# Layer 0 of a four-layer convolutional block: the pixel transposes become products with a diagonal of scales, with a second product for the biases

## The chip, the core and the metric

The kernel runs on one core of a Trainium2 chip. The metric is the time of one execution on the device in microseconds, as the median of the runs shown. The core has five engines with a queue each: TensorE (PE in the profile; PEld are its weight loads), VectorE (DVE), ScalarE (ACT), GpSimd (POOL) and SyncE (SP, which here only issues DMAs).

## The reference, cut to what matters

The input x is one image of 1024 channels by 64 x 64 pixels in float32. Four layers each add their output to x, and each first normalizes its input over 32 groups of 32 channels (`_gn`). Layers 1 and 3 are products with a 1024 x 1024 matrix and a bias, layer 2 is three products around a scan over the pixels. Only layer 0 is touched in substance:

```
x_norm = _layernorm2d(_gn(x), ln_w, ln_b)      # per channel, over its 64 x 64 pixels
dt     = softplus(einsum('bsdc,c->bsd', x_norm, dt_w) + dt_b)
log_a  = dt * -exp(log_A)                      # per channel and image row
M      = exp(cums[t] - cums[j]) for j <= t     # cums: running sum over the channels
x      = x + einsum('btjr,bjrc->btrc', M, x_norm)
```

So layer 0 is, for every pixel, a linear recurrence over the 1024 channels, out[t] = a[t] out[t-1] + x_norm[t], in which a depends on the channel and on the image row. The two normalizations of a channel fold into one scale and one bias per channel; ln_w and ln_b are a scale and a bias per pixel.

## The kernel before

**Tiling of layer 0.** The image is taken in eight units u of two channel tiles (256 channels, one chunk c) by half the pixels (2048); u counts chunk 0 low half, chunk 0 high half, chunk 1 low half and so on. `low[c]` and `image` hold the halves in SBUF with channels on partitions. The recurrence runs along channels, so pixels must come to the partitions: a unit is cut into four pieces, and each piece i (32 in all) covers four tiles of 128 pixels by 256 channels.

**What happens to a piece.** `normalize(n)` on ScalarE writes the scaled and shifted channels of a quarter of a unit to a tile xn (L563; two calls for every two pieces). `turn_in(i)` transposes them with TensorE, eight 128 x 128 transposes with `ident` into two PSUM tiles (L578), and VectorE (L584) or ScalarE (L586) writes them to `XT[i]`, applying the pixel's ln_w and ln_b; the argument `share` says which of the four are VectorE's. `row_dt(i)` accumulates the products for dt of a unit in `PD[u]` (L594). `decay(u, step)` turns a finished PD into the factors `A[u]` (ScalarE L603 to L612, VectorE L609). `scan(i)` is four recurrences on VectorE (L620), `hand_on(i)` keeps the last column for the next chunk, `turn_back(i)` transposes back into PSUM (L634), and `add_up(i)` adds that to the image and keeps the sums (L644). `unit_stats` takes the statistics of a unit that is still to come (L542), `norm_chunk(c)` works out scale and bias of a chunk in steps with two small products (gn_pg L198, gn_pv L207), and `squares` takes sums of squares of the finished pixels on ScalarE (L659).

**The order.** It is written by hand: layer 0 runs under a manual schedule, so every engine executes its instructions in the order in which the Python text emits them. Before the loop, chunk 0 is normalized, seven pieces are turned in (LEAD = 7) and unit 0 gets its decay. Then piece i of the loop emits scan(i), add_up(i - 1), turn_in(i + 7), row_dt(i + 6), turn_back(i), with the statistics of later units in pieces 0 to 3 and 8 to 11 and the decay of the next unit in every fourth piece. The PSUM tiles of turn_in ("tp") and of turn_back ("pb") are double buffered; small products of the normalization use "tp" too. GpSimd meanwhile sums blocks of the weights of later layers (L445 to L448), with its own DMAs.

**Layers 1 and 2** use a Strassen-like scheme with seven products (L832) on sums of blocks: `b_sets` is a generator whose steps are spread between the products, plain blocks b21, b11, b22, then t1 = b12 - b11, t2 = b22 - t1, t3 = t2 - b11 and t4 = b21 - t2, each as four subtractions of 128 x 512 (L790), t2 on VectorE for the first pair and on GpSimd (or the engine given) for later ones. The products come in the order b21, b11, b22, t2, t3, t1, t4.

Of the kernel before, what the change touches and what calls it, by code (L numbers as in the profile page):

```python
# [9 lines left out]
F32 = mybir.dt.float32  # L10
# [8 lines left out]
P = 128  # L19
C = 1024  # L20
HW = 64
# [69 lines left out]
def tile_net(ctx: ExitStack, tc: tile.TileContext, x, par_d, cst_d, w_d, w2_d, dbcw_d, out):  # L91
# [5 lines left out]
    def ps_tp(name):  # L97
        return psum.tile([P, FB], F32, tag="tp", name=name)
# [57 lines left out]
    def finish_of(steps):  # L156

        while True:
            try:
                next(steps)  # L160
            except StopIteration as stop:
                return stop.value
# [336 lines left out]
    with tc.issue_after(exp_ln.ins), tc.tile_pool(name="l0x", bufs=2) as lx, \  # L499
# [7 lines left out]
        def half(u):  # L507

            c, h = divmod(u, 2)
            return image[:, c * CH : (c + 1) * CH, :] if h else low[c]  # L510
# [27 lines left out]
        def unit_stats(u, some):  # L538
            c, h = divmod(u, 2)
            for j in some:  # L540
                k, i = divmod(j, 4)
                nc.vector.bn_stats(stats[:, c * CH + k, 4 * h + i, :], half(u)[:, k, i * FB : (i + 1) * FB])  # L542
# [8 lines left out]
            nc.vector.tensor_scalar_mul(nmean0[:, at], mean, -1.0)  # L551
            norms[c] = yield from norm_steps(f"gn0_{c}", mean, var, CH, layernorm=True)

        xn, XT, PD, A, dt, PB = {}, {}, {}, {}, {}, {}

        def normalize(n):

            u, j = divmod(n, 4)
            q, k = divmod(j, CH)
            scale, bias = norms[u // 2]  # L560
            xn[n] = l0.tile([P, 2, TR, HW // 4], F32, tag=f"xn{k}", name=f"xn{n}")
            part = half(u)[:, k, :].rearrange("p (r a g w) -> p a g r w", r=TR, a=2, g=2)[:, q]
            nc.scalar.activation(xn[n], part, AF.Identity, bias=bias[:, k : k + 1], scale=scale[:, k : k + 1])  # L563

        def tile_in(u, t, k):
            v = xn[4 * u + CH * (t // 8) + k].rearrange("p g r w -> p (g r w)")
            return v.rearrange("p (g b j) -> p g j b", g=2, j=4)[:, t // 4 % 2, t % 4]

        def turn_in(i, share, tag="tp"):

            u, g = divmod(i, NPIECE)
            XT[i] = l0.tile([P, 4, CH * P], F32, tag="xt", name=f"xt{i}", bufs=10)
            for b in range(2):
                pt = (psum if tag == "tp" else ps0).tile([P, FB], F32, tag=tag, name=f"xpt{i}_{b}")
                for j in range(2):
                    t = 4 * g + 2 * b + j
                    for k in range(CH):
                        nc.tensor.transpose(pt[:, (CH * j + k) * P : (CH * j + k + 1) * P],  # L578
                                            tile_in(u, t, k), ident)
                for j in range(2):  # L580
                    at = (u % 2) * T0 + 4 * g + 2 * b + j
                    to, ps = XT[i][:, 2 * b + j, :], pt[:, j * CH * P : (j + 1) * CH * P]
                    if 2 * b + j in share:
                        nc.vector.tensor_scalar(to, ps, pcol("lnw", at), pcol("lnb", at), ALU.mult, ALU.add)  # L584
                    else:
                        nc.scalar.activation(to, ps, AF.Identity, bias=pcol("lnb", at), scale=pcol("lnw", at))  # L586

        def row_dt(i):
            u, g = divmod(i, NPIECE)
            if g == 0:  # L590
                PD[u] = ps0.tile([P, FB], F32, tag="pd", name=f"pd{u}")
            for j in range(4):
                t = 4 * g + j
                nc.tensor.matmul(PD[u][:, : CH * P], dtm[:, t, :], XT[i][:, j, :], start=(t == 0), stop=(t == T0 - 1))  # L594
# [42 lines left out]
        def add_up(i):  # L637
            u, g = divmod(i, NPIECE)
            c, h = divmod(u, 2)
            for k in range(CH):  # L640
                part = half(u)[:, k, :].rearrange("p (r g q j) -> p g r q j", r=TR, g=4, q=4)[:, g]
                at = h * NPIECE + g
                ps = PB[i][k].rearrange("p (j r q) -> p r q j", j=4, r=TR)
                nc.vector.scalar_tensor_tensor(part, ps, 1.0, part, ALU.mult, ALU.add,  # L644
                                               accum_out=sum0[:, c * CH + k, at : at + 1])

        def squares(u, j, g=None):

            c, h = divmod(u, 2)
            k, q = divmod(j, 2)  # L650
            ct = c * CH + k
            junk = l0.tile([P, HN // 2], BF16, tag="junk", name=f"junk{u}_{j}_{g}", bufs=1)
            if g is None:
                part, at = half(u)[:, k, q * HN // 2 : (q + 1) * HN // 2], h * NPIECE + q
            else:
                part = half(u)[:, k, :].rearrange("p (r w) -> p r w", r=TR)[:, :, 16 * g : 16 * g + 16]
                at = h * NPIECE + g
                junk = junk[:, :FB].rearrange("p (r w) -> p r w", r=TR)
            nc.scalar.activation(junk, part, AF.Square, bias=nmean0[:, ct : ct + 1], accum_out=sq0[:, ct, at : at + 1])  # L659

        sums = (None for m in (W1, WX) for _ in sum_weights(m, wsum0, nc.gpsimd, lag=(1, 0)))
# [11 lines left out]
            next(chain)  # L673
            score(4)
        finish_of(chain)
        for n in range(4):
            normalize(n)
        unit_stats(2, range(4))
        turn_in(0, range(4))
        turn_in(1, range(4), "pb")  # L680
        for _ in scores:
            pass
        row_dt(0)
        turn_in(2, (1, 3))
        row_dt(1)
        turn_in(3, (1, 3), "pb")
        row_dt(2)
        unit_stats(2, range(4, 8))
        unit_stats(3, range(4))
        row_dt(3)  # L690
        decay(0, 0)
        normalize(4)
        unit_stats(3, range(4, 8))
        chain = norm_chunk(1)
        decay(0, 1)
        decay(0, 2)
        next(chain)
        normalize(5)
        turn_in(4, ())
        next(chain)  # L700
        row_dt(4)
        next(chain)
        normalize(6)
        normalize(7)
        turn_in(5, ())
        row_dt(5)
        turn_in(6, ())
# [1 line left out]
                8: [(7, range(4))], 9: [(7, range(4, 8))], 10: [(6, range(4))], 11: [(6, range(4, 8))]}  # L709
        for i in range(NI):  # L710
            u, g = divmod(i, NPIECE)
            if i > 0 and i + LEAD + 2 < 4 * NU:
                normalize(i + LEAD + 2)
            scan(i)
            hand_on(i)
            if i == 0:
                finish_of(chain)
                chain = iter(())
            if g == 3 and u + 1 < NU:
                decay(u + 1, 1)  # L720
                decay(u + 1, 2)
            if i > 0:
                add_up(i - 1)
            if i + LEAD < NI:
                turn_in(i + LEAD, ())
            if i + LEAD - 1 < NI:
                row_dt(i + LEAD - 1)
            turn_back(i)
            if i == 0:
                normalize(LEAD + 1)  # L730
                normalize(LEAD + 2)
            if u + 1 < NU and g == 2:
                decay(u + 1, 0)
            for v, some in todo.get(i, ()):
                unit_stats(v, some)
            if i in (3, 11):
                chain = norm_chunk(2 if i == 3 else 3)
            next(chain, None)
            if i >= NPIECE:
                squares(u - 1, g)  # L740
            if u == NU - 1 and 0 < g:
                for k in range(CH):
                    squares(u, 2 * k, g - 1)
            if g == 0 and u % 2 == 1:
                last_keep = keep(u // 2)
            if i == 2 * NPIECE:
                bring(6)
            next(sums, None)
# [28 lines left out]
    def b_sets(B, make, first=False, eng=None):  # L777

        def plain(name, row, col, upto=KH):
            B.setdefault(name, [])  # L780
            for k in range(len(B[name]), upto):
                t = b_tile(name, k, B["name"])
                make(t, row * KH + k, col)
                B[name].append(t)

        def comb(name, one, two, ks, eng):
            if name not in B:
                B[name] = [b_tile(name, k, B["name"]) for k in range(KH)]
            for k in ks:
                eng.tensor_tensor(B[name][k], B[one][k], B[two][k], ALU.subtract)  # L790

        slow = nc.vector if first else eng or nc.gpsimd
        plain("b21", 1, 0)
        yield
        plain("b11", 0, 0)
        yield
        plain("b22", 1, 1)
        yield
        for upto in (2, KH):
            plain("t1", 0, 1, upto)  # L800
            comb("t1", "t1", "b11", range(upto - 2, upto), nc.vector)
            yield
        comb("t2", "b22", "t1", range(KH), slow)
        yield
        for name, one, two in (("t3", "t2", "b11"), ("t4", "b21", "t2")):
            for ks in ((0, 1), (2, 3)):
                comb(name, one, two, ks, eng or nc.gpsimd)
                yield
# [987 lines left out]
```

## Time and profile before

| | us |
|---|---|
| median of three runs | 2735.31 (2735.19 to 2739.77) |
| the profiled execution, its own time | 2736.82 |
| its span, first to last instruction | 2735.0 |
| mean granted TensorE clock in it | 0.983 |
| TensorE matmul busy | 2613.8 (96%) |
| VectorE busy | 1804.5 (66%) |
| ScalarE busy | 1089.8 (40%) |
| GpSimd busy | 1224.4 (45%) |
| first scan of layer 0 starts (L620) | 52.37 |
| first product of layer 1 starts (L832) | 222.48 |

Times inside the profile count from the first instruction. The page cuts the span into 40 slices of 68 us with the busy share of each engine in tenths. A line of a group or of the timeline names the source line, the engine, the operation, output<-inputs, partitions x elements and the count. In the timeline the first column is the start and the second the length of the merged stretch; what stands in square brackets is the idle time before it and the instruction that ended it. Ends of matmuls are modelled, so TensorE is best read from start to start.

### The profile page before, as it was taken

The numbers are of one execution on the slowest core, as the hardware profiler recorded it, in microseconds if no ns is written. First come the engines' busy times: TensorE is split into PE (matmuls) and PEld (weight loads), VectorE is DVE, ScalarE is ACT, GpSimd is POOL, SyncE is SP. The second block draws the span as 40 slices with busy tenths as digits, with TensorE's granted clock in tenths as the row PEclk, the third lists the DMA queues.
The fourth block names the chain that finished last, engine by engine and source line by source line (L and its number), as shares of the span: only waits on it lengthen the run. The fifth ranks groups of instructions, "written<-read, shape, count | busy, mean of one in ns | idle before, by whom it ended". The sixth has DMA issues, their size and how long they took to land.

```text
span 2735.0 us, 30900 instructions
## 1 busy us (share of the span) xinstructions
PE 2613.8 (96%) x9594; PEld 1726.7 (63%) x9594; DVE 1804.5 (66%) x3793; ACT 1089.8 (40%) x1840; POOL 1224.4 (45%) x1103
## 2 busy tenths in 40 slices
PE   4778999999999999999999999999999999999999
PEld 3664444444555555544444447888888888788887
DVE  7996765555445565477777665567576676777777
ACT  4783110104655654475757554322233133221220
POOL 4154224421112002357475655556575565555544
PEclk9998999999999999999999999999999999999999
DMA  7345557645433434587767874879899898788896
GB/s 286 119 166 185 175 206 262 202 131 202 162 106 107 138 129 102 162 267 223 228 195 226 274 222 144 243 246 304 217 277 292 239 304 234 251 289 294 298 328 214
DMA packets 423448, 591.46 MB, mean 216 GB/s; under 512 B 149973, under 2 KB 211541, under 8 KB 420214
## 3 DMA queue, kind: packets, MB, share of 16 engines
q1 hardware_dynamic: 298934, 365.76, 41.9%
q10 hardware_dynamic: 91456, 136.33, 14.2%
q0 software_dynamic: 32896, 87.40, 12.5%
q8 instruction: 78, 1.28, 0.2%
q14 instruction: 84, 0.69, 0.1%
HBM read 432.02 MB, written 157.36 MB: 215 GB/s over the span
## 4 chain that ended last, share of the span: by engine, by line
PE 47%; DMA 4%; POOL 3%; issue 3%; DVE 2%; ACT 1%; SPq 0%; POOLq 0%; DVEq 0%; ACTq 0%
PE mm L832 8%; PE q_P6P L1670 5%; PE q_P5P L1670 5%; PE q_P7P L1670 5%; PE q_P2P L1670 5%; PE q_P4P L1670 5%; PE q_P3P L1670 5%; PE q_P1P L1670 5%; DMA y_d<-y,dst 2%; PE py L1319 1%; POOL s L461 1%; PE pg L1302 1%; POOL t L790 1%; DMA g<-tok_d,src 0%; PE pr L1280 0%
## 5 line engine op out<-in xcount | busy, mean ns | idle before, releaser
L832 PE MATMUL mm<-t,w 128*128 128x512 f32 x1536 | 685.2, 597 | 4.6 <-POOL t L790 4.0
L832 PE MATMUL mm<-b,w 128*128 128x512 f32 x1152 | 516.4, 599 | 4.0 <-ACT b L936 2.9
L832 PEld LDWEIGHTS mm<-t,w 128*128 128x128 f32 x1536 | 286.7, 191 | 332.0 <-issue 318.1
L832 PEld LDWEIGHTS mm<-b,w 128*128 128x128 f32 x1152 | 216.8, 192 | 255.1 <-issue 243.7
L1328 POOL DMA_INDIRECT y_d<-y,dst x74 | 73.7, 996 | 184.6 <-ACT y L1324 107.4
L1055 DVE SCALAR_TENSOR_TENSOR cvp<-xs,par,cvp 128x512 f32<-128x512 f32 x128 | 95.3, 754 | 77.9 <-ACT cvp L1052 75.7
L1639 ACT COPY qQ<-q_P5P 128x512 f32<-128x512 f32 x48 | 28.1, 585 | 290.4 <-PE q_P5P L1670 239.5
L1082 POOL TENSOR_TENSOR acc<-l2xt,acc 128x136 f32<-128x136 f32 x56 | 28.2, 504 | 236.9 <-ACT l2xt L1076 233.6
L461 POOL TENSOR_TENSOR s<-s 128x256 f32<-128x256 f32 (+3 forms) x120 | 130.2, 1092 | 7.9
L790 POOL TENSOR_TENSOR t<-b,t 128x512 f32<-128x512 f32 x72 | 92.9, 1318 | 72.2 <-DVE t L790 48.1
L1322 ACT COPY g<-py 8x512 f32<-8x512 f32 x146 | 83.8, 574 | 95.0 <-PE py L1319 92.0
L1106 DVE TENSOR_TENSOR xs<-mm,xs 128x512 f32<-128x512 f32 x64 | 41.8, 684 | 117.8 <-PE mm L832 117.8
L951 DVE SCALAR_TENSOR_TENSOR image<-mm,par,image 128x512 f32<-128x512 f32 x64 | 47.2, 747 | 104.4 <-PE mm L832 104.3
L1310 DVE TENSOR_TENSOR E<-E,pg 128x512 f32<-128x512 f32 x74 | 50.7, 685 | 76.0 <-PE pg L1302 66.2
L1074 PEld LDWEIGHTS l2pt<-both,cv 128*128 128x128 f32 x512 | 77.2, 191 | 35.6 <-issue 24.6
L1438 ACT ACTIVATE qb<-x_x_b,gn_bias,gn_r_r 128x512 f32<-128x512 f32 x64 | 48.9, 806 | 113.9 <-DVE qQ L1600 50.5
L1670 PE MATMUL q_P4P<-t_t,wq_P4P 128*128 128x256 f32 x384 | 93.9, 389 | 0.0
L936 ACT ACTIVATE b<-image,gnl_bias,gnl_r_r 128x512 f32<-128x512 f32 x48 | 37.2, 809 | 138.1 <-PE mm L832 111.5
L1670 PE MATMUL q_P5P<-t_t,wq_P5P 128*128 128x256 f32 x384 | 90.8, 379 | 0.0
L1670 PE MATMUL q_P1P<-t_b,wq_P1P 128*128 128x256 f32 x384 | 90.6, 379 | 0.1
L1670 PE MATMUL q_P6P<-t_t,wq_P6P 128*128 128x256 f32 x384 | 90.7, 379 | 0.0
L1670 PE MATMUL q_P7P<-t_t,wq_P7P 128*128 128x256 f32 x384 | 90.7, 379 | 0.0
(415 smaller groups left out, 5914.6 us busy)
## 6 DMA issues: line engine op xcount, KB each, us to landing
w<-s_d SPq DMA_DIRECT2D x96, 512.0 KB
w<-in_w_dram SPq DMA_DIRECT2D x72, 512.0 KB
x_x_b<-x_d ACTq DMA_DIRECT2D x28, 1024.0 KB
image<-x_d SPq DMA_DIRECT2D x12, 2048.0 KB
wq_P6P<-s_d SPq DMA_DIRECT2D x84, 256.0 KB
wq_P7P<-s_d SPq DMA_DIRECT2D x84, 256.0 KB
wq_P5P<-s_d SPq DMA_DIRECT2D x84, 256.0 KB
wq_P3P<-s_d SPq DMA_DIRECT2D x84, 256.0 KB
```

The lines of the kernel that those rows point to most:

```text
L461: eng.tensor_tensor(out, a, b, ALU.subtract)
L790: eng.tensor_tensor(B[name][k], B[one][k], B[two][k], ALU.subtract)
L832: nc.tensor.matmul(to[o], w[:, k, o * P : (o + 1) * P], B[name][k], start=(fresh and k == 0), stop=(k == KH - 1), skip_group_check=True)
L951: nc.vector.scalar_tensor_tensor(part, ps, pcol(bias_name, o), part, ALU.add, ALU.add)
L1055: nc.vector.scalar_tensor_tensor(cv, xo[:, at + t : at + t + FB], pcol("dww", 3 * o + t), cv, ALU.mult, ALU.add)
L1074: nc.tensor.matmul(pt[:, q * NV : (q + 1) * NV], cv[:, (q0 + q) * P : (q0 + q + 1) * P], both[:, o, :], start=True, stop=True)
L1106: nc.vector.tensor_tensor(part, ps, part, ALU.add)
L1310: nc.vector.tensor_tensor(Ef, Ef, pg, ALU.mult)
L1322: nc.scalar.copy(rows[k + 1][h * LC : h * LC + S, :DH], py[h * LC : h * LC + S])
L1328: nc.gpsimd.indirect_dma_start(out=y_d[:, :], out_offset=bass.IndirectOffsetOnAxis(ap=dst_[:, k : k + 1], axis=0), in_=y[:, :], in_offset= ...
L1438: nc.scalar.activation(tile_of(j, name)[:, k], held[j, "x", name][:, k], AF.Identity, bias=bias, scale=scale)
L1670: nc.tensor.matmul(ps[:, o, :], w[:, k, o * P : (o + 1) * P], rhs[:, k, :], start=(new and o == 0 and k == 0), stop=(k == 1), skip_group_c ...
```

## The change

`normalize` and its tiles xn go away. Instead `norm_operands(c)` makes, for each chunk, two operands: `spread`, for each channel tile a 128 x 128 diagonal with the channel's scales (two ScalarE activations of `ident`), and `shift`, the 256 biases as a row, split into three bfloat16 terms on partitions 0, 32 and 64 (a ScalarE copy, two small f32 products and five VectorE operations). `turn_in` then multiplies the raw pixels, as stationary operand, by `spread`, as moving operand, and adds a product of a tile of ones with `shift` into the same PSUM tile. The pixels of a tile are now those with the same index modulo 16, read straight from the image with a step of 16 elements; the order of the pixel constants and the access patterns of `add_up` and `squares` follow. In the lead-in, pieces 0 and 1 are evacuated by VectorE and ScalarE half and half, and the statistics of unit 2 move behind row_dt(3); the operands of chunks 1, 2 and 3 are made in pieces 0, 6 and 14. In `b_sets` the first two of t2's four subtractions are emitted in the step before.

```diff
-        def normalize(n):
...
-            nc.scalar.activation(xn[n], part, AF.Identity, bias=bias[:, k : k + 1], scale=scale[:, k : k + 1])
+        ones = l0.tile([96, P], BF16, name="ones", bufs=1)
+        nc.gpsimd.memset(ones, 0.0)
+        for q in range(3):
+            nc.gpsimd.memset(ones[32 * q : 32 * q + 1, :], 1.0)
+        three = l0.tile([P, CH, 96], F32, name="three", bufs=1)
+        nc.gpsimd.memset(three, 0.0)
+        spread, shift = {}, {}
+
+        def norm_operands(c):
+            scale, bias = norms[c]
+            nc.scalar.copy(three.rearrange("p k (q z) -> p k q z", q=3)[:, :, :, 0],
+                           bias.unsqueeze(2).to_broadcast([P, CH, 3]))
+            spread[c] = l0.tile([P, CH, P], F32, tag="spread", name=f"spread{c}")
+            for k in range(CH):
+                nc.scalar.activation(spread[c][:, k, :], ident, AF.Copy, scale=scale[:, k : k + 1])
+            row = ps_tp(f"row{c}")[:96, : CH * P]
+            for k in range(CH):
+                nc.tensor.matmul(row[:, k * P : (k + 1) * P], three[:, k, :], ident, start=True, stop=True)
+            parts = shift[c] = l0.tile([96, CH * P], BF16, tag="parts", name=f"parts{c}")
+            rest = l0.tile([96, CH * P], F32, tag="rest", name=f"rest{c}", bufs=1)
+            nc.vector.tensor_copy(parts, row)
+            nc.vector.tensor_tensor(rest[:64], row[:64], parts[:64], ALU.subtract)
+            nc.vector.tensor_copy(parts[:64], rest[:64])
+            nc.vector.tensor_tensor(rest[:32], rest[:32], parts[:32], ALU.subtract)
+            nc.vector.tensor_copy(parts[:32], rest[:32])
 
         def tile_in(u, t, k):
-            v = xn[4 * u + CH * (t // 8) + k].rearrange("p g r w -> p (g r w)")
-            return v.rearrange("p (g b j) -> p g j b", g=2, j=4)[:, t // 4 % 2, t % 4]
+            return half(u)[:, k, t : HN : T0]
...
-                        nc.tensor.transpose(pt[:, (CH * j + k) * P : (CH * j + k + 1) * P],
-                                            tile_in(u, t, k), ident)
+                        nc.tensor.matmul(pt[:, (CH * j + k) * P : (CH * j + k + 1) * P], tile_in(u, t, k),
+                                         spread[u // 2][:, k, :], start=(j == 0 and k == 0), stop=False,
+                                         skip_group_check=True)
+                for j in range(2):
+                    nc.tensor.matmul(pt[:, CH * j * P : CH * (j + 1) * P], ones, shift[u // 2], start=False,
+                                     stop=(j == 1), skip_group_check=True)
...
-                part = half(u)[:, k, :].rearrange("p (r g q j) -> p g r q j", r=TR, g=4, q=4)[:, g]
+                part = half(u)[:, k, :].rearrange("p (m g j) -> p g m j", g=NPIECE, j=4)[:, g]
...
-        for n in range(4):
-            normalize(n)
-        unit_stats(2, range(4))
-        turn_in(0, range(4))
-        turn_in(1, range(4), "pb")
+        norm_operands(0)
+        turn_in(0, (1, 3))
+        turn_in(1, (1, 3), "pb")
         for _ in scores:
             pass
+        turn_in(2, (1, 3))
         row_dt(0)
-        turn_in(2, (1, 3))
+        turn_in(3, (1, 3), "pb")
         row_dt(1)
-        turn_in(3, (1, 3), "pb")
         row_dt(2)
-        unit_stats(2, range(4, 8))
+        row_dt(3)
+        unit_stats(2, range(8))
         unit_stats(3, range(4))
-        row_dt(3)
         decay(0, 0)
...
             if i == 0:
                 finish_of(chain)
+                norm_operands(1)
                 chain = iter(())
...
+            if i in (6, 14):
+                norm_operands(2 if i == 6 else 3)
...
         for upto in (2, KH):
             plain("t1", 0, 1, upto)
             comb("t1", "t1", "b11", range(upto - 2, upto), nc.vector)
+            if upto == KH:
+                comb("t2", "b22", "t1", range(2), slow)
             yield
-        comb("t2", "b22", "t1", range(KH), slow)
+        comb("t2", "b22", "t1", range(2, KH), slow)
         yield
```

More of the change, by code (lines that the diff above doesn't have):

```diff
@@ L552, in norm_chunk @@
             norms[c] = yield from norm_steps(f"gn0_{c}", mean, var, CH, layernorm=True)
-        xn, XT, PD, A, dt, PB = {}, {}, {}, {}, {}, {}
-        def normalize(n):
[L558 to L562, printed above, removed]
-            nc.scalar.activation(xn[n], part, AF.Identity, bias=bias[:, k : k + 1], scale=scale[:, k : k + 1])
+        XT, PD, A, dt, PB = {}, {}, {}, {}, {}
+        ones = l0.tile([96, P], BF16, name="ones", bufs=1)
[22 more added lines that the diff above has]
+            nc.vector.tensor_copy(parts[:32], rest[:32])
         def tile_in(u, t, k):
-            v = xn[4 * u + CH * (t // 8) + k].rearrange("p g r w -> p (g r w)")
-            return v.rearrange("p (g b j) -> p g j b", g=2, j=4)[:, t // 4 % 2, t % 4]
+            return half(u)[:, k, t : HN : T0]
         def turn_in(i, share, tag="tp"):
@@ L640, in add_up @@
             for k in range(CH):
-                part = half(u)[:, k, :].rearrange("p (r g q j) -> p g r q j", r=TR, g=4, q=4)[:, g]
+                part = half(u)[:, k, :].rearrange("p (m g j) -> p g m j", g=NPIECE, j=4)[:, g]
                 at = h * NPIECE + g
-                ps = PB[i][k].rearrange("p (j r q) -> p r q j", j=4, r=TR)
+                ps = PB[i][k].rearrange("p (j m) -> p m j", j=4)
                 nc.vector.scalar_tensor_tensor(part, ps, 1.0, part, ALU.mult, ALU.add,
@@ L655, in squares @@
             else:
-                part = half(u)[:, k, :].rearrange("p (r w) -> p r w", r=TR)[:, :, 16 * g : 16 * g + 16]
+                part = half(u)[:, k, :].rearrange("p (m g j) -> p g m j", g=NPIECE, j=4)[:, g]
                 at = h * NPIECE + g
-                junk = junk[:, :FB].rearrange("p (r w) -> p r w", r=TR)
+                junk = junk[:, :FB].rearrange("p (m j) -> p m j", j=4)
             nc.scalar.activation(junk, part, AF.Square, bias=nmean0[:, ct : ct + 1], accum_out=sq0[:, ct, at : at + 1])
@@ L675, in tile_net @@
         finish_of(chain)
-        for n in range(4):
-            normalize(n)
-        unit_stats(2, range(4))
-        turn_in(0, range(4))
-        turn_in(1, range(4), "pb")
+        norm_operands(0)
+        turn_in(0, (1, 3))
+        turn_in(1, (1, 3), "pb")
         for _ in scores:
             pass
+        turn_in(2, (1, 3))
         row_dt(0)
-        turn_in(2, (1, 3))
+        turn_in(3, (1, 3), "pb")
         row_dt(1)
-        turn_in(3, (1, 3), "pb")
         row_dt(2)
-        unit_stats(2, range(4, 8))
+        row_dt(3)
+        unit_stats(2, range(8))
         unit_stats(3, range(4))
-        row_dt(3)
         decay(0, 0)
-        normalize(4)
         unit_stats(3, range(4, 8))
@@ L697, in tile_net @@
         next(chain)
-        normalize(5)
         turn_in(4, ())
@@ L702, in tile_net @@
         next(chain)
-        normalize(6)
-        normalize(7)
         turn_in(5, ())
@@ L711, in tile_net @@
             u, g = divmod(i, NPIECE)
-            if i > 0 and i + LEAD + 2 < 4 * NU:
-                normalize(i + LEAD + 2)
             scan(i)
@@ L728, in tile_net @@
             turn_back(i)
-            if i == 0:
-                normalize(LEAD + 1)
-                normalize(LEAD + 2)
             if u + 1 < NU and g == 2:
@@ L1757, in pixels @@
     def pixels(a):
-        return a.reshape(2, TR, 4, 4, 4).transpose(1, 3, 0, 2, 4).reshape(P, 2 * T0)
+        return a.reshape(2, TR, TW, T0).transpose(1, 2, 0, 3).reshape(P, 2 * T0)
     par[:, PAR["logA"]] = np.repeat(g["L0_conv_log_A"].reshape(2, TR), TW, axis=1).T
@@ L1762 @@
     par[:, PAR["lnb"]] = pixels(g["L0_conv_ln_b"])
-    par[:, PAR["dtw"]] = np.tile(g["L0_conv_dt_w"].reshape(4, TW, 4).transpose(1, 0, 2).reshape(TW, T0), (TR, 1))
+    par[:, PAR["dtw"]] = np.tile(g["L0_conv_dt_w"].reshape(TW, T0), (TR, 1))
     par[:, PAR["dtb"]] = rows(g["L0_conv_dt_b"])
```

## The prediction

> **What bounds the kernel now.** I start from the slices of the page, because shares of the whole span hide that layer 0 differs from the rest.
>
> ```profile
> PE   4778999999999999999999999999999999999999
> DVE  7996765555445565477777665567576676777777
> PEclk9998999999999999999999999999999999999999
> ```
>
> A slice is 68 us. After layer 0 (slices 1 to 3) TensorE is full, so a microsecond gained or lost in layer 0 should reach the end whole. The table of windows inside layer 0:
>
> ```profile
> 100.00:120.00 20.00, 15.59 (x93) 12.95 (x92) 19.02 (x38) 19.28 (x34) 5.78 (x10) 0.97 0.44 159
> 160.00:180.00 20.00, 17.88 (x106) 14.95 (x106) 16.25 (x34) 19.94 (x39) 10.05 (x17) 1.00 0.56 211
> ```
>
> Columns: PE, PEld, DVE, ACT, POOL busy, clock, DMA. VectorE fills the first window, ScalarE both; TensorE's busy figure is inflated by pipelining, so I price it by start to start in the timeline:
>
> ```profile
> 97.92 1.12 PE L578 MATMUL xpt<-cst,xn 128*128 128x128 f32 x8
> 98.88 1.89 PE L594 MATMUL pd<-xt,dtm 128*128 128x256 f32 x8
> 100.61 1.04 PE L634 MATMUL pb<-cst,xt 128*128 128x128 f32 x8
> ...
> 653.37 1.26 PE L1074 MATMUL l2pt<-both,cv 128*128 128x162 f32 x8
> 654.47 3.60 PE L832 MATMUL mm<-t,w 128*128 128x512 f32 x8
> ```
>
> One piece i costs TensorE 0.96 (turn_in, 8 transposes, one record each) + 1.73 (row_dt, 4 products, two records each: an f32 product runs as two passes) + 0.87 (turn_back; 8 records to the next group, as in other pieces) = 3.56 us. VectorE's piece is scan to scan:
>
> ```profile
> 150.15 2.67 DVE L620 TENSOR_TENSOR_SCAN xt<-a,carry,xt 128x256 f32<-128x256 f32 x4
> 153.94 2.67 DVE L620 TENSOR_TENSOR_SCAN xt<-a,carry,xt 128x256 f32<-128x256 f32 x4
> ...
> 64.70 0.69 DVE L644 SCALAR_TENSOR_TENSOR low<-pb,low 128x512 f32<-128x512 f32 x1 [4.04 <-PE pb L634]
> ```
>
> 3.79 us, or 6.16 in the eight pieces with four bn_stats (107.69 to 113.85). ScalarE needs 4.06: evacuation 1.80, squares 1.13, normalize 1.13. So VectorE bounds pieces 0 to 3 and 8 to 11, ScalarE with the decay steps the others, and TensorE has slack everywhere. VectorE's waits between 60.7 and 182 sum to 12.4 us; the 4.04 above is the largest.
>
> The clock matters at the head:
>
> ```profile
> 44.00:48.00 4.00, 0.00 (x0) 0.00 (x0) 4.00 (x9) 1.55 (x3) 1.59 (x3) 0.88 0.66 231
> 48.00:52.00 4.00, 3.16 (x13) 2.50 (x13) 0.96 (x7) 3.00 (x6) 2.15 (x2) 0.50 0.28 104
> ```
>
> TensorE idles from 42.5 to 48.4 and comes back at half clock.
>
> **What the Trainium skill says.** (1) "TensorE: Matmul & The Clock Gate", LDWEIGHTS: a load takes columns / 1.2 GHz, 107 ns for 128; the trace agrees: 0.87/8 = 109 ns for turn_back. (2) "SBUF — State Buffer", Door 1: lines are 16 bytes, and an access that crosses to a new line pays. The old transposes load with a step of 16 bytes and take 0.96/8 = 120 ns, so it shows; the new step is 64 bytes, also a line per element, and no run here shows that step. (3) The first page, Part 1: the clock falls to half after an idle window of about 3.4 us, and rises after a busy one; the windows above agree on the fall, while the rise took until 57.4. (4) The same page, weight-path modes: non-f32 weights of 128 columns load fast; no row here shows it.
>
> **The change, part by part.**
>
> *Removed:* 32 normalize on ScalarE (L563, 39.1 us busy, 1.13 us of each piece). It stops being a bound: 4.06 becomes 2.93.
>
> *turn_in:* 256 one-pass transposes become 256 f32 products of two passes, plus 128 bf16 bias products with a weight load each. A pass: streaming gives 1.10/8 = 137 ns at 162 columns (L1074), hence 109 at 128; the strided load gives 120. I take 120; bounds 109 and 175 [...]. A bf16 product of 256 columns: half of a 216 ns f32 pass, 108; bounds 50 and 220. So 16 x 0.120 + 4 x 0.108 = 2.35, +1.39 us a piece, and TensorE's piece becomes 4.95. That exceeds VectorE's 3.79 plus about 0.7 for the decay steps: TensorE becomes the bound of the pieces without statistics.
>
> *norm_operands, four times:* ScalarE one copy and two 128x128 activations (about 0.2 + 2 x 0.3, estimate from 417 ns for 256 columns); TensorE four passes, 0.5; VectorE five small operations, nearest rows 0.51 (L584, PSUM) and 0.41 (L609): about 1.9 us. Behind them in VectorE's queue stand statistics and the next scan.
>
> *Head.* Before: bias at 28.0, first scan at 52.37, third at 68.32. After, by each engine's order of instructions: row product and diagonal by 28.9, parts to 30.7; the first bias product waits for them; turn_in 0 to 2 end at 36.9, row_dt(0) 38.6, turn_in(3) 41.0, row_dt 1 to 3 46.2. Evacuations are shared, so VectorE is not the limit, but all 16 statistics now follow them: 41.5 + 16 x 0.61 = 51.3. Then m and aggregates, 52.3. TensorE has idled six microseconds, so turn_in(4) runs cold: 16 x 0.213 + 4 x 0.213 = 4.3 us; the gn_pv product behind it ends at 57.6, and the first scan starts at 58.1 (+5.7). Worse follows: the parts of chunk 1 wait for a row product that stands behind row_dt(4), turn_in(5), row_dt(5) and turn_in(6) on TensorE, and its operand behind the evacuation of turn_in(6) on ScalarE: 57.6 + 1.9 + 2.4 + 1.7 + 2.4 + 1.9 = 67.9. VectorE idles from 61.5; parts 69.9, statistics 72.4, scan(1) to 75, add_up and statistics, scan(2) at 78.7: +10.4.
>
> *Loop.* Pieces 2, 3: VectorE-bound as before; scan(4) at 92.5 against 81.68, +10.8. Pieces 4 to 7: TensorE 4 x 4.95 + 0.5, and before scan(7) the parts of chunk 2 wait for a row product behind turn_back(6): scan(8) at 114.6 against 101.52, +13.1. Pieces 8 to 11: 6.16 against 4.95, VectorE hides all, still +13.1 at scan(12), 140.4. Pieces 12 to 24, the last with a turn_in: 140.3 + 13 x 4.95 + 0.8 (gn_pv, row) + 0.6 = 206.1; add_up(24), then scan(26) at 207.5 against 190.02: +17.5. The last pieces have no turn_in and are VectorE-bound in both. Sum about +18.
>
> *Costed at nothing.* The new pixel order in add_up and squares: runs of four elements are still a line each (bounds -1 and +6 if 64 operations of 0.68 slow by 15%). Five memsets on GpSimd sit before DMAs whose data is not wanted for 10 us. SP's queue is unchanged.
>
> *T2:* as many subtractions, two of four a step earlier. In layer 1 GpSimd's order comes out the same, so its one long wait stays:
>
> ```profile
> 465.88 7.36 PE L832 MATMUL mm<-t,w 128*128 128x512 f32 x12 [4.01 <-POOL t L790]
> ```
>
> That is the pair behind a weight sum (t4), not T2. In the WR stage two 1.24 us subtractions move ahead of weight sums, gathers and scatters; TensorE's waits there total 13 us, nearly all for gathers and G. I take 0, bounds -3 and +3.
>
> Against the profiled execution (span 2735.0, own time 2736.8) this makes 2754.8; it lies 1.5 above the median 2735.3, so the forecast is 2753.
>
> **Rivals.**
> (A) *The above*, chance 0.58: +13 to +23.
> (B) *The 64-byte step is slower than 16 bytes*: at 175 ns a pass turn_in costs 3.2, a piece 5.8. Seventeen pieces and seven turn_ins of the head add 0.85 each, 20 more: about 2773, and to 2795 if a pass takes 240. For it: the old step already costs 11 ns; against: the line is already one per element. Chance 0.18.
> (C) *The head is shorter*, TensorE warm at 52 and row products overtaken by nothing: 5 to 8 less, 2745. The half clock at 48.00 speaks against it. Chance 0.11.
> (D) *VectorE stays the bound*: the waits of 12.4 us were ScalarE's normalize; if turn_in costs under 1.7 us, TensorE's piece is under 4.3, those waits go, less 3.8 for parts in the loop: 2735.3 - 8.6 + 2 of head, 2729. All f32 products in the trace take two passes, which speaks against. Chance 0.08.
> (E) *Head loss and ScalarE relief cancel*, 2737, 0.05. That the edit does nothing is excluded: both queues differ.
>
> **Numbers.** Within 0.2% (5.5 us) is about what a measurement of this kernel can tell from none. Slower: A, B and most of C, 0.86; same 0.06; faster 0.08. For eight in ten the range holds A, most of C and half of B: 2742 to 2780.
>
> **What would show it.** Right: TensorE start to start 2.2 to 2.5 us per turn_in; scans 4.9 to 5.0 apart in pieces 12 to 24; scan(2) near 79; first L832 product near 240 instead of 222.5; no normalize rows. Wrong: VectorE full over pieces 12 to 24 and TensorE waiting; turn_in over 3 us (B) or under 1.7 (D); a clock of 1.0 at 52 (C); any loss that arises after the first L832 product.

## The result, and the profile after

| | us |
|---|---|
| before, median of four runs | 2735.25 (2734.11 to 2739.77) |
| after, median of four runs | 2797.01 (2795.98 to 2800.52) |
| ratio after / before | 1.0225, 95% interval 1.0207 to 1.0243 |
| forecast | 2753, range 2742 to 2780 |

The direction was right and the size was not: the change costs 62 us where 18 were forecast. The span of the profiled execution grew from 2735.0 to 2795.6 us. The first product of layer 1 (L848, which was L832) starts at 280.38 instead of 222.48, so 57.9 of the 60.5 us arise in layer 0 and 2.6 behind it. The slices of the page for the changed kernel show where the bound moved:

```profile
PE   5997999999999999999999999999999999899998
DVE  5677567355445555377777766658577585777776
PEclk9998999999999999999999999999999999999999
```

TensorE is now full in slices 1 and 2 (9 and 9, where it was 7 and 7), and VectorE shows 6, 7, 7 in slices 1 to 3, where it showed 9, 9, 6. Inside layer 0, the table of windows (columns as before: PE, PEld, DVE, ACT, POOL, clock, DMA):

```profile
160.00:180.00 20.00, 18.83 (x106) 17.79 (x106) 14.15 (x35) 8.54 (x18) 7.74 (x11) 1.00 0.42 159
200.00:220.00 20.00, 20.00 (x111) 19.07 (x111) 12.44 (x26) 11.32 (x23) 9.86 (x15) 1.00 0.34 113
```

ScalarE fell from 19.94 to 8.54 in the window from 160 to 180, as forecast, and VectorE, with 14.15 of 20 us busy, has waits; TensorE is busy for 18.83 us of that window and for the whole of the later one. The price of a piece is in TensorE's timeline (start, length, and what it ran):

```profile
209.81 1.91 PE L596 MATMUL xpt<-spread,low 128*128 128x128 f32 x8
211.55 0.38 PE L600 MATMUL xpt<-parts,ones 96*128 96x256 bf16 x2
211.78 1.91 PE L596 MATMUL xpt<-spread,low 128*128 128x128 f32 x8
213.52 0.39 PE L600 MATMUL xpt<-parts,ones 96*128 96x256 bf16 x2
213.74 1.89 PE L616 MATMUL pd<-xt,dtm 128*128 128x256 f32 x8
215.47 1.04 PE L656 MATMUL pb<-cst,xt 128*128 128x128 f32 x8
216.34 1.91 PE L596 MATMUL xpt<-spread,low 128*128 128x128 f32 x8
```

From start to start, eight passes of products with the diagonal take 1.74 us, which is 218 ns a pass; the two bias products take 0.22. Twice that is 3.93 for turn_in; with row_dt (1.73) and turn_back (0.87) a piece is 6.53. The scans on VectorE follow it, where they came every 3.79 us before:

```profile
197.74 2.67 DVE L642 TENSOR_TENSOR_SCAN xt<-a,carry,xt 128x256 f32<-128x256 f32 x4
204.26 2.67 DVE L642 TENSOR_TENSOR_SCAN xt<-a,carry,xt 128x256 f32<-128x256 f32 x4
```

In all, TensorE's work from 60.1 to the end of turn_back(25) at 251.6 is 28 turn_ins, 28 row_dts and 26 turn_backs: 28 x 3.93 + 28 x 1.73 + 26 x 0.87 = 181 of 191 us. TensorE has hardly a wait in this stretch, so it bounds layer 0 nearly throughout. That holds in the pieces with statistics too, since 6.53 exceeds VectorE's 6.16: there VectorE is full as well (scans 6.16 apart from 134.37 on), because it makes up for a stall just before them; in the run late below, with a shorter stall, these scans come 6.53 apart.

### The profile page after: what moved, and what is told of

The parts are those of the page before. It is cut to its first block, busy times and chain, and to the rows that moved or that the text cites. A ratio compares the mean times of both kernels' runs of the same rounds, so it can differ in the third digit from the quotient of the medians.

```text
span 2795.6 us, 31693 instructions
## 1 busy us (share of the span) xinstructions
PE 2695.3 (96%) x9994; PEld 1816.1 (65%) x9994; DVE 1813.9 (65%) x3809; ACT 1062.7 (38%) x1824; POOL 1222.2 (44%) x1108
## 4 chain that ended last, share of the span: by engine, by line
PE 52%; DVE 2%; POOL 1%; DMA 1%; issue 1%; ACT 1%; SPq 0%; DVEq 0%; POOLq 0%; ACTq 0%
PE mm L848 10%; PE q_P2P L1686 5%; PE q_P6P L1686 5%; PE q_P1P L1686 5%; PE q_P5P L1686 5%; PE q_P3P L1686 5%; PE q_P7P L1686 5%; PE q_P4P L1686 5%; PE py L1335 2%; PE pg L1318 2%; DMA g<-tok_d,src 1%; PE pr L1296 1%; DMA y_d<-y,dst 1%; POOL s L461 0%; POOL t L804 0%
## 5 line engine op out<-in xcount | busy, mean ns | idle before, releaser
L848 PE MATMUL mm<-t,w 128*128 128x512 f32 x1536 | 685.0, 597 | 4.5 <-POOL t L804 4.5
L848 PE MATMUL mm<-b,w 128*128 128x512 f32 x1152 | 516.3, 599 | 4.0 <-ACT b L952 2.9
L848 PEld LDWEIGHTS mm<-t,w 128*128 128x128 f32 x1536 | 286.9, 191 | 331.5 <-issue 319.3
L848 PEld LDWEIGHTS mm<-b,w 128*128 128x128 f32 x1152 | 217.0, 192 | 254.9 <-issue 243.8
L608 ACT ACTIVATE xt<-xpt,par 128x256 f32<-128x256 f32 x120 | 61.3, 560 | 102.3 <-PE xpt L600 102.3
L1686 PE MATMUL q_P2P<-t_b,wq_P2P 128*128 128x256 f32 x384 | 90.7, 379 | 0.0
```

What stands on the lines that cost most here:

```text
L848: nc.tensor.matmul(to[o], w[:, k, o * P : (o + 1) * P], B[name][k], start=(fresh and k == 0), stop=(k == KH - 1), skip_group_check=True)
L1686: nc.tensor.matmul(ps[:, o, :], w[:, k, o * P : (o + 1) * P], rhs[:, k, :], start=(new and o == 0 and k == 0), stop=(k == 1), skip_group_c ...
```

## Experiments

Times of the kernel before on the same chips were 2734.0, 2735.7 and 2736.3 in the three series. "Layer 0" below is the start of the first large product, from one profile; "behind" is what the span has left after it.

| kernel | time, us | ratio to before | layer 0 | behind |
|---|---|---|---|---|
| before | 2735.25 | 1 | 222.5 | 2512.6 |
| after | 2797.01 | 1.0225 | 280.4 | 2515.2 |
| step4 | 2771.4 (one run) | | 252.2 | 2517.3 |
| step8 | 2770.5 (one run) | | 251.2 | 2517.4 |
| step16 | 2803.7 | 1.0247 (1.0231 to 1.0264) | 285.1 | 2516.3 |
| turn64 | 2751.1 (one run) | | 231.1 | 2518.1 |
| identmov | 2796.5 (one run) | | 279.0 | 2515.5 |
| nobias | 2786.7 (two runs) | 1.0183 (1.0163 to 1.0203) | 267.7 | 2517.5 |
| late | 2802.7 | 1.0239 (1.0222 to 1.0256) | 285.4 | 2516.2 |
| late4 | 2766.7 (two runs) | 1.0110 (1.0090 to 1.0130) | 246.8 | 2517.3 |
| t2only | 2744.0 | 1.0035 (1.0023 to 1.0047) | 224.6 | 2514.9 |
| not2 | 2790.8 | 1.0196 (1.0182 to 1.0210) | 282.6 | 2507.1 |
| lean | 2740.2 | 1.0017 (1.0008 to 1.0026) | 230.5 | 2506.7 |
| bpool | 2731.6 | 0.9987 (0.9980 to 0.9993) | 218.9 | 2513.1 |

### Why a pass takes 218 ns: step16, step4, step8, turn64, identmov

The first question was whether the step of 64 bytes, the product, or its moving operand makes the pass slow. The edit of the step kernels, with s = 4, 1 and 2 elements:

```diff
         def tile_in(u, t, k):
-            return half(u)[:, k, t : HN : T0]
+            s = 4
+            at = t // s * P * s + t % s
+            return half(u)[:, k, at : at + (P - 1) * s + 1 : s]
```

> Left as in the changed kernel but for the pixels of a tile: tile t is read as 128 pixels with a step of 4 elements (16 bytes) inside a run of 512, so the values that are turned are other pixels and the output is not the reference's; number, kind and order of instructions are unchanged. Theory S (the weight load of a pass slows with the step of 64 bytes): a pass falls from 218 to about 120 ns, a half piece of L596 from 1.74 to 0.96 us, TensorE's piece from 6.53 to about 4.95, first large product near 240 us instead of 280, time 2750 to 2762. Theory R (an f32 product with a diagonal as moving operand costs 218 ns a pass wherever its tile lies): nothing changes, 2797.

> Same edit with a step of one element, so that a tile is 128 neighbouring pixels (output again not the reference's). S: a pass costs about 109 ns as in turn_back; 1 to 4 us less than with 16 bytes. R: 218 ns a pass and 2797 us.

> As step4 and step16, with a step of two elements (8 bytes; other pixels are turned, so the output is not the reference's). Theory L (a load of an f32 product pays for each 16-byte line it touches): half as many lines as with 16 bytes, so about 112 to 120 ns a pass, time near step4's 2771. Theory E (any step other than one element halves the load): 218 to 233 ns, near 2797 to 2803. Between them, 160 to 175 ns, if the cost grows with the bytes stepped over.

turn64 keeps the step and puts a plain transpose of one pass in the place of each product; the scales and the bias products are left out:

```diff
-                        nc.tensor.matmul(pt[:, (CH * j + k) * P : (CH * j + k + 1) * P], tile_in(u, t, k),
-                                         spread[u // 2][:, k, :], start=(j == 0 and k == 0), stop=False,
-                                         skip_group_check=True)
-                for j in range(2):
-                    nc.tensor.matmul(pt[:, CH * j * P : CH * (j + 1) * P], ones, shift[u // 2], start=False,
-                                     stop=(j == 1), skip_group_check=True)
+                        nc.tensor.transpose(pt[:, (CH * j + k) * P : (CH * j + k + 1) * P],
+                                            tile_in(u, t, k), ident)
```

> Changed kernel with plain transposes of the raw pixels at the step of 64 bytes in place of the products, bias products left out, so the scale and bias of the norm are missing from the output; half as many passes. S: a transpose takes about 218 ns where the kernel before shows 120, 0.87 us for four tiles of two channel blocks; TensorE's piece about 4.35, time 2745 to 2758. R: a transpose takes 120 ns, 0.48 us, piece 3.56, time 2730 to 2745.

identmov puts `ident` in the place of `spread[u // 2][:, k, :]` and keeps all else:

> Changed kernel with the identity as moving operand in the place of the diagonal of scales (the scale is left out of the output; pixels, step, passes and bias products kept). If the pass is slow because of how the stationary tile is loaded: 218 ns a pass and 2797 within 4. If the diagonal of scales as moving operand is part of it: a pass of about 113 ns as in turn64, time near 2771.

The timelines of TensorE, two lines of each: start to start over eight passes gives the pass. step4 (0.89 us for eight, 112 ns each):

```profile
175.74 1.06 PE L598 MATMUL xpt<-spread,image 128*128 128x128 f32 x8
176.63 0.38 PE L602 MATMUL xpt<-parts,ones 96*128 96x256 bf16 x2
```

step8 (0.95, 118 ns):

```profile
175.05 1.10 PE L598 MATMUL xpt<-spread,image 128*128 128x128 f32 x8
176.00 0.38 PE L602 MATMUL xpt<-parts,ones 96*128 96x256 bf16 x2
```

step16 (1.87, 233 ns):

```profile
173.42 2.03 PE L598 MATMUL xpt<-spread,image 128*128 128x128 f32 x8
175.29 0.38 PE L602 MATMUL xpt<-parts,ones 96*128 96x256 bf16 x2
```

turn64 (0.91, 113 ns for a transpose that reads the same pixels with the same 64 bytes between them as the changed kernel):

```profile
170.16 1.07 PE L596 MATMUL xpt<-cst,low 128*128 128x128 f32 x8
171.07 1.89 PE L612 MATMUL pd<-xt,dtm 128*128 128x256 f32 x8
```

identmov (1.74, 218 ns for a product of the same two operands, pixels 64 bytes apart and `ident`, that turn64 transposes in 113):

```profile
170.18 1.91 PE L596 MATMUL xpt<-cst,image 128*128 128x128 f32 x8
171.92 0.38 PE L600 MATMUL xpt<-parts,ones 96*128 96x256 bf16 x2
```

So a pass of an f32 product costs, by the distance of the elements of its stationary operand (the one that is loaded as weights):

| bytes from element to element | f32 product, ns a pass | transpose, ns |
|---|---|---|
| 4 | 112 (step4) | 109 (turn_back) |
| 8 | 118 (step8) | |
| 16 | 233 (step16) | 120 (turn_in before) |
| 64 | 218 (after, identmov) | 113 (turn64) |

Both theories of the first series fell, S by step16 and R by step4: it isn't the 64 bytes as such, and it isn't the product as such. It is the two together, an f32 product whose stationary elements lie 16 bytes apart or more. (turn64's time, 2751, lies in the range of theory S, though its pass came out as R said: the time alone would have misled.) That the moving operand holds scales has no part in it (identmov, 218).

The Trainium skill ("SBUF — State Buffer", Door 1) says that lines are 16 bytes and that at least two hits to a line are needed for full bandwidth. The four products fit this: 8 bytes, two hits, 118 ns; 16 bytes, one hit, about twice that. It leaves open why 16 bytes cost 15 ns more than 64, and its remark that four fp32 can be stepped over for free doesn't hold for the product at 16 bytes. The transposes don't fit: at one hit a line they lose 4 to 11 ns. The lines name the pixels second in both, `spread,low` and `cst,low`, as the operand that is loaded; that a transpose loads them as a product does is read from this order alone. Why it escapes is not settled here.

What it is worth: from after to step4 and step8 the time falls by 26 us, and layer 0 by 28.

### What the bias product costs: nobias

The two products of `ones` with `shift` in each half of turn_in are left out and `stop` moves to the last product of the half.

> Changed kernel without the 128 bias products (the bias of the norm is left out of the output). TensorE-bound: the 28 turn_ins behind the head give back 28 x 0.44 = 12 us, head 3 more as two groups ran at half clock there and the first no longer waits for the parts: 2780 to 2786. If something else bounds the pieces: less than 5 us.

Layer 0 ended 12.6 us earlier and the time fell by 10.3, to just above the range expected. A turn_in takes 3.5 us instead of 3.93, from start to start:

```profile
139.11 3.66 PE L596 MATMUL xpt<-spread,low 128*128 128x128 f32 x16
142.61 1.89 PE L613 MATMUL pd<-xt,dtm 128*128 128x256 f32 x8
```

So the 0.44 us are work on the path, but the gain is not 28 times that. The head gained more than the 3 us expected, 4.9 at the first scan (60.70 against 65.56) and 5.1 at scan(2), and what follows gained only 7.6. In pieces 8 to 11 nothing was gained (from scan(8) to scan(12) 25.8 us in both kernels): with 6.1 us a piece TensorE is below VectorE's 6.16 there.

### The stalls of norm_operands: late, late4

In the loop of the changed kernel VectorE stands still three times for a row product, here for chunks 1 and 2 (start, length; in brackets the wait and what ended it):

```profile
78.47 0.42 DVE L578 CAST parts<-row 96x256 bf16<-96x256 f32 x1 [9.63 <-PE row L575]
...
115.42 2.42 DVE L642 TENSOR_TENSOR_SCAN xt<-a,xt 128x256 f32<-128x256 f32 x4
...
128.41 0.42 DVE L578 CAST parts<-row 96x256 bf16<-96x256 f32 x1 [5.76 <-PE row L575]
...
130.29 2.41 DVE L642 TENSOR_TENSOR_SCAN xt<-a,xt 128x256 f32<-128x256 f32 x4
```

scan(7) comes 14.9 us after scan(6), and so does scan(15) after scan(14). It looks like a loss of some 16 us. The edit takes the parts out of the way of those scans:

```diff
+            if i in (7, 15):
+                norm_operands(2 if i == 7 else 3)
             if i + LEAD < NI:
                 turn_in(i + LEAD, ())
...
-            if i in (6, 14):
-                norm_operands(2 if i == 6 else 3)
```

> Changed kernel with norm_operands for chunks 2 and 3 called one piece later, ahead of turn_in(14) and turn_in(22), so that on VectorE the parts follow add_up and no longer stand ahead of scan(7) and scan(15) (each was 14.9 us after the scan before it). If TensorE bounds these pieces (6.53 us each, hardly a wait between 60 and 245 us), the stalls on VectorE are covered: 2797 within 3. If they are on the path: 8 to 16 us less, 2781 to 2789.

> The same move in step4 (tiles of neighbouring pixels, output not the reference's), where a piece costs TensorE 4.83 us and scan(7) and scan(15) come 11.5 us after the scans before them, 6 us more than in the kernel before. If these stalls let TensorE run dry and its clock drop: the first large product 4 to 10 us ahead of step4's 252.2, time 2761 to 2767. If TensorE's work is the bound there too: within 2 of 252.2 and 2770.

In late the step from scan(6) to scan(7) shrank from 14.9 to 7.1 us, and nothing was won: 2802.7, layer 0 longer by 5.0. The stall was covered by TensorE's queue. The small loss, outside the 3 us that were allowed for it (though the intervals of the two ratios overlap), has a place in TensorE's waits of after, and of late below it (us in total, times, longest), from 60 to 290 us:

```profile
PE row L575 <- ACT three L568: 1.2, 1, 1.2
```

```profile
PE row L575 <- ACT three L568: 4.4, 3, 1.6
```

One piece later the row product reaches TensorE before ScalarE has written its operand, and an engine that bounds the stage now waits twice more. In late4, where a piece costs TensorE only 4.83, the same edit ends layer 0 at 246.8 instead of 252.2, 5.4 us earlier. Of these, 1.3 were already there at scan(2), ahead of what was moved; about 4 are left for the stall, which was on the path there.

### The T2 edit: t2only, not2

> Kernel before with the T2 edit alone. Theory T (the 2.5 us that the changed kernel loses after its layer 0 come from the moved subtractions): +2 to +4 us, 2737 to 2739, with the loss in the stage of the gathers between 1220 and 1600 us. Theory N (the loss comes from transfers that meet the later phase of layer 0 otherwise): 2735 within 1.5 us.

> Changed kernel with the T2 edit undone, the rest kept. If the loss of T2 (t2only: ratio 1.0035, L790 on VectorE 3.09 us for a pair instead of 1.28 beside GpSimd's early pair) adds up with the new layer 0: 4 to 10 us less than 2797, so 2787 to 2793. If that loss belongs to the phase in which t2only met its gathers, and not to the edit: 2797 within 2.

The edit was costed at nothing. It costs 9.6 us alone (2735 x 0.0035, interval 6.3 to 12.9), more than the 2 to 4 expected, and undoing it in the changed kernel takes 6 off. The column "behind", from single profiles, points the same way: 2514.9 to 2518.1 in the ten with the edit, 2506.7 to 2513.1 in the four without. But the size differs: 2.4 from before to t2only (whose profile is of its fastest execution), 8.0 from not2 to after. So the 2.6 us that the changed kernel loses behind layer 0 are a balance. Without the edit it gains 5.4 us there (not2 2507.1 against 2512.6 before; lean the same), and where that gain comes from is not traced.

The place is in the stage of layer 2 in which gathers and products alternate. First VectorE's timeline of the kernel before, at a pair of t1's subtractions:

```profile
1362.86 1.28 DVE L790 TENSOR_TENSOR t<-t,b 128x512 f32<-128x512 f32 x2
```

with TensorE's product that waits for VectorE's G behind it:

```profile
1366.45 1.10 PE L1319 MATMUL py<-g,G 128*128 128x512 f32 x2 [0.26 <-DVE G L1315]
```

and then t2only's timelines of VectorE, GpSimd and TensorE at the same work:

```profile
1364.61 3.09 DVE L790 TENSOR_TENSOR t<-t,b 128x512 f32<-128x512 f32 x2
...
1364.04 2.50 POOL L790 TENSOR_TENSOR t<-b,t 128x512 f32<-128x512 f32 x2
...
1369.99 1.10 PE L1321 MATMUL py<-g,G 128*128 128x512 f32 x2 [2.04 <-DVE G L1317]
```

Emitted in the same step, GpSimd's early pair of t2 and VectorE's second pair of t1 start together. GpSimd begins first and is done at 1366.54. Of VectorE's pair the first subtraction alone takes 2.48 us, to 1367.09: about the length of an undisturbed one (0.69) after GpSimd's end. So VectorE stood still until GpSimd was through. The Trainium skill describes this ("SBUF — State Buffer", the section on the two separate sides): VectorE with two SBUF inputs and a GpSimd operation that reads SBUF take one port pair as an exclusive lock for a whole instruction, and the other blocks. Here the block covers both of GpSimd's instructions. Behind the pair in VectorE's queue stands G, and TensorE waits 2.04 us for it where it waited 0.26 before. This happens twice in t2only (at 1364 and 1512 us) and three times in the changed kernel (at 1270, 1422 and 1570; at 1422.55 the pair takes 3.08 us and TensorE waits 2.04). Between 1200 and 1700 us TensorE's waits for G add up to 9.4 us in t2only against 5.6 before, and to 8.7 in the changed kernel against 4.3 in not2. That explains about 4 us of the 6 to 10; the rest is not traced.

### What is left: lean, bpool

lean is turn64 with the T2 edit undone and the move of late.

> turn64 (plain transposes of the raw pixels, scale and bias left out of the output) with the T2 edit undone and norm_operands moved as in late: all that was found put right, and turn_in as cheap as a turn of the image can be. Sum of the parts: 2751 - 6 - 4 = 2741. If these parts do not add up, 2746 to 2751. Under 2733 if the relief of ScalarE (39 us of normalize) is worth something once turn_in is cheap.

The sum came out at 2740.2, and with a turn_in as cheap as a turn of the image can be, and no scale or bias, the kernel is still not faster than before. Its layer 0 is 8 us longer: scan(2) starts at 72.35 instead of 68.32, and scan(17) at 161.46 instead of 150.15, of which a part is made good later. VectorE's waits in lean from 60 to 225 us show where a part of it lies:

```profile
DVE parts L578 <- PE row L575: 6.5, 3, 5.6
```

One wait of 5.6 us is that of chunk 1 in the head, and the five operations on the parts take 1.9 us of VectorE for each chunk. norm_operands has its price even where the turning has none; how much of the 8 us it is, and how much the new order of the lead-in, no run separates.

A smaller relief of ScalarE is to be had from the kernel before:

```diff
-            nc.scalar.activation(xn[n], part, AF.Identity, bias=bias[:, k : k + 1], scale=scale[:, k : k + 1])
+            if n >= 8 and n % 2:
+                nc.gpsimd.tensor_scalar(xn[n], part, scale[:, k : k + 1], bias[:, k : k + 1], ALU.mult, ALU.add)
+            else:
+                nc.scalar.activation(xn[n], part, AF.Identity, bias=bias[:, k : k + 1], scale=scale[:, k : k + 1])
```

> Kernel before with the normalize of every second piece from the ninth on (12 of 32) given to GpSimd as one tensor_scalar. Relief theory: ScalarE's piece falls from 4.06 to about 3.5 us, the three waits for a of about 1 us each and the late decay steps shrink, 3 to 8 us less, 2727 to 2732. Collision theory: GpSimd's 1.3 us slow VectorE beside it as in t2only (1.8 us for a pair), 12 times 1 us, and xn arrives late: 2738 to 2748.

2731.6 is 0.13% less than before, with an interval that excludes no change, though under the 0.2% that was taken as the limit. VectorE's waits between 60 and 220 us, of before and then of bpool:

```profile
DVE m L609 <- ACT e L606: 3.4, 4, 1.5
DVE xt L620 <- ACT a L612: 2.9, 3, 1.1
```

```profile
DVE xt L623 <- ACT a L615: 0.9, 1, 0.9
```

The waits for the decay steps go from 6.3 to 0.9, and layer 0 is 3.6 us shorter. The feared collision hardly showed. Beside one of GpSimd's 1.19 us operations a small VectorE operation on two SBUF tiles (L203) took 0.89 us instead of 0.16. But `scan` and `add_up` read one of their two tiles from PSUM, so they don't have the two SBUF inputs of the block above, and the scans kept their spacing of 3.79. By about 4 us it is the only one of these kernels that is faster than the kernel before.

## Why the prediction was wrong in size

**The bound moved as argued.** TensorE becomes the bound of the pieces without statistics, ScalarE falls away, VectorE waits: right, and the decision that the change would be slower rested on it. "Any loss that arises after the first L832 product" was named as a sign of error, and there is one.

**The step that failed: "the strided load gives 120. I take 120".** The 120 ns came from transposes at a step of 16 bytes and was carried to products. A product's load at that step takes 233, and 218 at 64. The bounds, 109 and 175, were too low as well. The term 16 x 0.120 measured 16 x 0.218; the bias term, 4 x 0.108 = 0.43, measured 0.44. turn_in is 3.93 instead of 2.35, a piece 6.53 instead of 4.95. At its place on the path this is 28 us of the 44 by which the forecast was short (after less step4 in layer 0). With 112 ns a piece is 4.83, so the rest of that sum holds.

**Rival B had the price and not the reason.** It reckoned 2773 at 175 ns and 2795 at 240 (its own 24 turn_ins of 16 passes make that 2799), and the sign set for it, a turn_in over 3 us, appeared. But it laid the cost on 64 bytes against 16, and its argument against itself, "the line is already one per element", is true and proves nothing: the old rows were transposes. Nor were their 11 ns a measure of what a line costs, since turn64's transposes lose only 4 at 64 bytes. The page that was cited for the line also says how many hits a line needs, and that half of the sentence was passed over.

**The head was 4 us short, and more with the slow loads.** scan(2) was forecast at 78.7 and came at 82.37 in step4, 88.85 after. Two of its terms are visible. Two of the five operations on the parts took 1.37 and 1.24 us instead of the 0.41 and 0.28 of later chunks, while GpSimd ran 1.3 us subtractions beside them. And the first groups of turn_in ran at half rate (a bias pair 0.42 us instead of 0.22, though the windows give a clock of 1.00 from 32 to 37), where only turn_in(4) was thought cold. The wait for the row product of chunk 1 was right in kind, with 71.3 in step4 and 77.8 after instead of 67.9.

**The loop was 8 us short even at 112 ns.** From scan(4) to scan(8) the forecast was 22.1 us and step4 shows 25.95; from scan(12) to scan(26) 67.1 and 72.75. late4 puts about 4 of it down to the place of norm_operands, which was priced at 0.8 to 2.3 for each chunk. The sum did not contain either that TensorE's clock falls inside the loop (what that costs no run shows): 0.57 from 96 to 104 us and 0.52 from 150 to 158 in step4, after the pieces in which VectorE lets it wait.

**T2: "I take 0, bounds -3 and +3".** Between 6 and 10 were measured; behind the layer 0 of the changed kernel the untraced gain of 5.4 hides most of it. GpSimd's order and TensorE's long wait for t4 were looked at (it stays, 4.5 us); who else works at the moment to which the subtractions move was not.

**The sum:** 28 us of passes, 12 of head and loop (252.2 less the forecast 240), 2.6 behind layer 0, about 43 of 44. The 12 are placed only in part. Nothing was lost in the new pixel order: an add_up takes 0.69 us as before.

## What to carry to other kernels

A duration belongs to an operation, its operands and their access pattern together: a transpose's load is no price for a product's load, and one row of each kind is to be found before a term is multiplied by some hundreds. Before a subtraction is moved to another step, look at which engine it will run beside: here VectorE stood still beside GpSimd when it read two tiles from SBUF, and not when one of them lay in PSUM. A long wait on an engine that is not the bound, even one that puts 15 us between two scans, can be worth nothing, and moving it may put a new wait on the engine that is.

## What was not expected of the hardware

The slow load does not follow TensorE's clock. Between 60 and 64 us the windows give the changed kernel a clock of 0.50, and its pass at 64 bytes takes there 1.86 / 8 = 232 ns, hardly more than 218:

```profile
60.52 2.07 PE L596 MATMUL xpt<-spread,image 128*128 128x128 f32 x8
62.38 0.64 PE L600 MATMUL xpt<-parts,ones 96*128 96x256 bf16 x2
```

At the same point step4, also at 0.50, takes 1.84 / 8 = 230 ns, twice its 112:

```profile
56.99 2.05 PE L598 MATMUL xpt<-spread,image 128*128 128x128 f32 x8
58.83 0.64 PE L602 MATMUL xpt<-parts,ones 96*128 96x256 bf16 x2
```

The next groups, still with slow bias pairs, say the same: 1.73 us for eight passes from 62.81 in the changed kernel, 1.71 from 59.26 in step4. At half clock the step thus costs nothing more, and at full clock the strided load keeps about the pace that the contiguous one has at half. So the slow load seems to be limited by something that TensorE's clock doesn't set; that is read from these places alone. It can't be the reading of such elements from SBUF as such, since turn64's transposes read them in 113 ns.
